# Two image layers on one core: VectorE in program order, loads a piece ahead, borders in the background, first group by channel pairs

## The chip, the cores and the metric

The kernel runs on one core of one Trainium2 chip. Its time is the device time of that core in microseconds; the median of three runs counts. TensorE (matmuls), VectorE, ScalarE (activations), GpSimd and SyncE (here it only issues DMA transfers) each work through a queue of their own.

## The reference

A batch of 32 images with 8 channels of 256 x 256 pixels, all f32, goes through two layers:

```python
def layer0(x):                      # x is normalised first: n = gn(x), 4 groups of 2 channels
    grid = n
    for _ in range(15):             # the "lattice": depthwise 3x3
        mapped = 3.9 * grid * (1 - grid)
        grid = 0.85 * (0.7 * mapped + 0.3 * conv3x3(mapped, K_local)) + 0.15 * n
    cml = clip(grid, 1e-4, 1 - 1e-4)
    h = relu(conv3x3(n, Wp, bp))    # 8 -> 128 channels
    nca = sigmoid(conv1x1(h, Wu, bu))
    g = relu(conv3x3(concat(n, cml, nca), Wg1, bg1))
    g = sigmoid(conv1x1(g, Wg2, bg2))
    return g * cml + (1 - g) * nca

y = x + layer0(gn(x))
qx = round(gn(y) * sx)              # sx = 127 / max|gn(y)|, over the whole batch
out = y + conv3x3(qx, qw) / (sx * sw) + bias
```

## The kernel before

Layer one works on groups of four images (`GB = 4`, eight groups). Four kinds of work run beside each other, and TensorE's order is written out by hand (each kind is a generator, and what it yields is its share of the time):

- **Preparation** (`normalise`, called by `prep`): a job is one image and two of its four channel pairs. `begin` loads each pair (`xr`, 512 KB) and takes its statistics at once (L305, L306); `scale` and `end` average them over the partitions with two small products on TensorE (`pm` L313, `pv` L324), get the deviation with a power on GpSimd (L327), normalise `xr` (L331), and make three copies: `xq` (ScalarE, L336), `hi` (VectorE, L342) and `lo` (GpSimd, L343). Six stores (L345, L352) write them at once to the scratch tensors `xq_s` and `xp_s`. One channel pair of one image is called a piece here. `hi`, `lo` and `xq` each have a single buffer, so each of them waits for the stores of the piece before.
- **Lattice** (`lattice`): for each of 8 channels, 15 steps of three tiles over the four images at once. A tile takes 12 products (L487) for two tensors, and on VectorE `gt` (L495) and the next `m_a` or `m_b` (L500). `m_a` gets rows of its neighbours with DMAs (`exchange`, L450, L451); `m_b`'s edge is masked on GpSimd (L504). The input of a channel comes from `xq_s` in 36 transfers (`load`).
- **NCA** (`nca`): per image, 3x3 products `ph` (L567), ReLU on ScalarE (L577), products `acc` (L584) and a sigmoid (L602), from `xp_s`, stored in `nc_s`.
- **Gate** (`gate`), one group behind: per image 10 pieces of two row blocks. `stage` loads `nb`, `cq` and `xb` (L671, L676, L690), rearranges `cq` to `cmb` on GpSimd (L681) and normalises `xb` to `xnb` on VectorE (L700); 18 products `pa` (L759), `pg` (L725), and `finish` with the gate's arithmetic (L730 to L735) and statistics (L743 to L745).

`together` emits one lattice step and then as much of the other three (the filler) as keeps both in proportion; `both` and `chain` mix the fillers. Before the first lattice, `prep(0, (0,))` prepares the first half (channel pairs 0 and 1) of four images; `prep(0, (1,))` follows beside the first lattice steps. The NCA of an image needs all its channels.

Only TensorE keeps this program order (L259). For VectorE, ScalarE, GpSimd and SyncE a planner sets the order at build time: it goes by the program's order among the instructions that it takes to be ready, by its own estimate of durations and transfers. On the chip each queue then runs in the order that was built.

Before all this, L194 to L202 store zeros to the border rows of 68 scratch tensors, four stores each, on ScalarE's DMA queue, from a tile `zt` in the pool `prep`. The pools of layer one (L261, L262) take over the space of `prep`. Layer two (L898 on) quantises the result and makes its convolution, image by image; the change doesn't touch it.

Of the kernel before, what the change touches and what calls it, by code (L numbers as in the profile page):

```python
# [31 lines left out]
F32 = mybir.dt.float32  # L32
# [8 lines left out]
P = 128  # L41
C = 8
# [71 lines left out]
def kernel(  # L114
# [46 lines left out]
    rstd_y = cp.tile([P, B], F32, name="rstd_y")  # L161
    dev_y = cp.tile([P, B], F32, name="dev_y")


# [7 lines left out]
    with tc.tile_pool(name="prep", bufs=1) as pp, tc.tile_pool(name="prep2", bufs=2) as pp2:  # L172
# [20 lines left out]

        zt = pp.tile([P, PW], F32, name="zt")  # L194
        G.memset(zt, 0.0)
        for t, n, w in (
            *((t, 2 * C, PW) for t in xp_s), *((t, C, W) for t in (*cm_s, *nc_s, *y_s))
        ):
            nc.scalar.dma_start(dram_ap(t, 0, [[w, n], [1, w]]), zt[:n, :w])
            for i in range(0, 11, 5):  # L200
                m = min(5, 11 - i) * n
                nc.scalar.dma_start(dram_ap(t, (257 + i) * n * w, [[w, m], [1, w]]), zt[:m, :w])  # L202

# [53 lines left out]
    with ExitStack() as one:  # L257

        one.enter_context(tc.manual_schedule(engines={mybir.EngineType.PE}))  # L259
        pool = lambda name, bufs, **kw: one.enter_context(tc.tile_pool(name=name, bufs=bufs, **kw))  # L260
        xp, sp2, gp, bp2, st = pool("xp", 4), pool("sp2", 1), pool("gp", 3), pool("bp2", 2), pool("st", 2)  # L261
        imp, hp, wk, wk1, np_ = pool("imp", 3), pool("hp", 12), pool("wk", 2), pool("wk1", 1), pool("np", 1)  # L262
        ps_c, ps_a = pool("ps_c", 6, space=PSUM), pool("ps_a", 2, space=PSUM)
# [24 lines left out]
        def normalise(jobs):  # L288

            def begin(b, half):
                xrs = []
                mv = st.tile([P, 2, 2], F32, name="mv", tag="mv")
                stats = st.tile([P, 2, 2, 6], F32, name="stats", tag="stats")
                for i in range(2):
                    g = 2 * half + i
                    xr = xp.tile([P, 2, 2, W], F32, name="xr", tag="xr")
                    nc.sync.dma_start(  # L300
                        xr.rearrange("p c h w -> p (c h) w"),
                        dram_ap(x, (b * C + 2 * g) * H * W, [[W, P], [P * W, 4], [1, W]]),
                    )
                    for j in range(2):
                        V.bn_stats(stats[:, i, j, :], xr[:, j].rearrange("p h w -> p (h w)"))  # L305
                    V.bn_aggr(mv[:, i, :], stats[:, i].rearrange("p j s -> p (j s)"))  # L306
                    xrs.append(xr)
                return b, half, xrs, mv

            def scale(b, half, xrs, mv):  # L310
                gs = slice(2 * half, 2 * half + 2)
                pm = ps_c.tile([P, 512], F32, name="pm", tag="pt")
                T.matmul(pm[:, 0:2], avg, mv[:, :, 0], start=True, stop=True)  # L313
                m, rstd = mean_x[:, b, gs], rstd_x[:, b, gs]
                V.tensor_copy(m, pm[:, 0:2])
                e = st.tile([P, 2], F32, name="e", tag="e")
                V.tensor_tensor(e, mv[:, :, 0], m, ALU.subtract)
                V.tensor_tensor(e, e, e, ALU.mult)
                V.tensor_tensor(e, e, mv[:, :, 1], ALU.add)
                return e  # L320

            def end(b, half, xrs, e):
                pv = ps_c.tile([P, 512], F32, name="pv", tag="pt")
                T.matmul(pv[:, 0:2], avg, e, start=True, stop=True)  # L324
                rstd = rstd_x[:, b, 2 * half : 2 * half + 2]
                V.tensor_scalar(rstd, pv[:, 0:2], GN_EPS, None, ALU.add)
                G.tensor_tensor(rstd, rstd, mhalf[:, 0:2], ALU.pow)  # L327
                for i, xr in enumerate(xrs):
                    g = 2 * half + i
                    flat = xr.rearrange("p c h w -> p (c h w)")  # L330
                    V.tensor_scalar(  # L331
                        flat, flat, mean_x[:, b, g : g + 1], rstd_x[:, b, g : g + 1],
                        ALU.subtract, ALU.mult,
                    )
                    xq = sp2.tile([P, 2, 2, 4, NJ], F32, name="xq", tag="xq")
                    S.activation(  # L336
                        xq.rearrange("p c h q j -> p (c h) q j"),
                        xr.rearrange("p c h (j q) -> p (c h) q j", q=4),
                        AF.Copy,
                    )  # L340
                    inner = lambda t: t[:, :, :, 1 : 1 + W]
                    V.tensor_copy(inner(hi), xr)  # L342
                    G.tensor_tensor(inner(lo), xr, inner(hi).bitcast(F32), ALU.subtract)  # L343
                    for h in range(2):
                        nc.sync.dma_start(  # L345
                            dram_ap(
                                xq_s[b % NBUF], (2 * g * H + P * h) * W, [[W, P], [H * W, 2], [1, W]]
                            ),
                            xq[:, :, h].rearrange("p c q j -> p c (q j)"),
                        )  # L350
                        for j, src in enumerate((hi, lo)):
                            nc.sync.dma_start(  # L352
                                dram_ap(
                                    xp_s[b % NBUF],
                                    (1 + P * h) * ROW + (C * j + 2 * g) * PW,
                                    [[ROW, P], [PW, 2], [1, PW]],
                                ),
                                src.bitcast(F32)[:, :, h, :],
                            )
                    yield 1.0  # L360
                ready.add((b, half))

            ahead = None
            for job in [*jobs, None]:
                now = begin(*job) if job else None
                yield 1.0
                if ahead:
                    e = scale(*ahead)
                    yield 1.0
                    yield from end(*ahead[:3], e)  # L370
                ahead = now

# [3 lines left out]
        def lattice(g):  # L376


            def load(u):


                c, out, dmas = u % C, [], []
                assert all((u // C * GB + i, c // 4) in ready for i in range(GB))
                for s in range(2):
# [57 lines left out]
            def background(n):  # L442
                for _ in range(min(n, len(later))):
                    nc.sync.dma_start(*later.pop(0))
                    issued[0] += 1

            def exchange(t, k):
# [109 lines left out]
        def nca(b):  # L557
# [80 lines left out]
            im = ahead  # L638
            if (b + 1, 0) in ready and (b + 1, 1) in ready:
                loaded[b + 1] = rows(b + 1, 0, 0)  # L640
# [26 lines left out]
        def stage(b, p, sc):  # L667
# [11 lines left out]
            )  # L679
            for k in range(n):  # L680
                G.tensor_copy(  # L681
                    cmb[:, k, 1 : 1 + W].rearrange("p (j q) -> p j q", q=4),
                    cq[:, k, :].rearrange("p (q j) -> p j q", q=4),
                )
            xb = bp2.tile([P, 2, W], F32, name="xb", tag="xb", bufs=3)
            if p in (0, 9):
                G.memset(xb, 0.0)
            for k in range(n):
# [6 lines left out]
                        [[W, r1_ - r0], [H * W, C], [1, W]],  # L695
                    ),
                )
            for k in range(n):
# [13 lines left out]
        def gate(b):  # L712
# [35 lines left out]
            last = done = None  # L748
            sc, ahead = staged.pop(b, None) or begin_gate(b)
            for p in range(10):  # L750
# [5 lines left out]
                for s, t in ((0, xnb), (1, cmb), (2, nb)):  # L756
# [11 lines left out]
                    if s < 2:  # L768
                        yield 2.6
                r1 = wk.tile([P, 512], F32, name="r1", tag="r1")  # L770
                S.activation(r1[:, : n * W], pa[:, : n * W], AF.Relu, bias=bv[:, 0:1])
# [93 lines left out]

        def prep(g, halves):
            return normalise([(b, half) for half in halves for b in range(g * GB, g * GB + GB)])

# [11 lines left out]
        T_NCA, T_GATE, T_PREP, T_LATTICE = 520.0, 340.0, 34.0, 8 * 45 * 1.97  # L880
        for _ in prep(0, (0,)):
            pass
        for g in range(NG):
            fill, t = images(nca, g), T_NCA
            if g:
                fill, t = both(fill, t, after(g - 1, images(gate, g - 1)), T_GATE), t + T_GATE
            if g + 1 < NG:
                fill, t = both(fill, t, prep(g + 1, (0, 1)), T_PREP), t + T_PREP
            if g == 0:
                fill, t = chain(prep(0, (1,)), fill), t + 20.0  # L890
            together(lattice(g), T_LATTICE, fill, t)
        for _ in images(gate, NG - 1):
            pass
# [115 lines left out]
```

## Time and profile before

| | |
|---|---|
| three runs | 14362.28, 14360.28, 14354.44 us |
| median | 14360.28 us |
| profiled run | 14414.7 us, mean TensorE clock 0.963 |

One run's profile is read here. Its first block gives the busy time of each engine. The second cuts the span in 40 slices of 360 us, with the busy tenths of each engine and the clock that TensorE was granted. The groups of instructions that matter for the change:

| group | count | mean ns | role |
|---|---|---|---|
| L487 `pt<-m_a`, `pt<-m_b` | 34560 | 497, 492 | lattice products |
| L567 `ph` | 24576 | 419, 402 | NCA products |
| L759 `pa` | 11520 | 588, 577, 576 | gate products |
| L495 `gt` | 5760 | 557, 549 | lattice, VectorE |
| L500 `m_a`, `m_b` | 5376 | 566, 575 | lattice, VectorE |
| L700 `xnb` | 608 | 493 | gate input, VectorE |
| L342 `hi` | 128 | 694 (median, first pieces) | preparation, VectorE |
| L343 `lo` | 128 | 2173 (median, first pieces) | preparation, GpSimd |

Matmuls overlap in the array, so the times of single ones add up to more than TensorE's busy time. Three more views are used: the chain of waits, which follows the work that ended last back from the end; the list of waits, which gives for each engine what ended its idle time (sum, times, longest); and a table of stretches of the run, with each engine's busy time, TensorE's clock and the DMA share in each.

### The profile page before, as it was taken

Reading aid. Unit: us, or ns where it says so; the run is one execution under the profiler, and the core shown is the slowest. Engines: PE = TensorE matmul, PEld = TensorE weight load, DVE = VectorE, ACT = ScalarE, POOL = GpSimd, SP = SyncE. Lnnn points to the kernel's source line nnn. Section 1 sums busy time; section 2 is a strip of 40 time slices with the busy share of each in tenths; the row PEclk is TensorE's granted clock in tenths of the full one; section 3 lists DMA queues with packets and bytes.
Section 4 is the critical chain, followed back from the end, with each engine's and each line's share of the span. In section 5 each row is a group of like instructions: output and inputs, shape, how many; then the busy total and the mean of one; then the engine's idle time right before and its main releaser. Section 6 shows DMA issues by size and latency. Waiting matters only on the chain.

```text
span 14414.7 us, 229163 instructions
## 1 busy us (share of the span) xinstructions
PE 13267.4 (92%) x81728; PEld 6423.3 (45%) x81728; DVE 8213.1 (57%) x16290; ACT 4039.8 (28%) x6274; POOL 2445.9 (17%) x4266
## 2 busy tenths in 40 slices
PE   2999999999999999999999999999999999999833
PEld 1554444444444444444444444444444444444311
DVE  3555555555555555555555555555555555555576
ACT  1333232232222222222322223222323222222122
POOL 1111111111111111111111111111111111112300
PEclk9999999999999999999999999999999999999966
DMA  5444444444444444444444434444444433333465
GB/s 148 93 97 92 90 103 106 103 94 100 110 94 100 99 106 94 103 100 95 100 103 107 98 93 106 110 94 94 104 104 98 103 88 88 80 83 78 122 195 176
DMA packets 2259559, 1496.74 MB, mean 104 GB/s; under 512 B 1061248, under 2 KB 2229504, under 8 KB 2258304
## 3 DMA queue, kind: packets, MB, share of 16 engines
q1 hardware_dynamic: 2176976, 1401.95, 41.9%
q10 hardware_dynamic: 81456, 80.12, 1.7%
q8 instruction: 664, 10.88, 0.3%
q14 instruction: 463, 3.79, 0.1%
HBM read 866.48 MB, written 478.69 MB: 93 GB/s over the span
## 4 chain that ended last, share of the span: by engine, by line
PE 70%; DMA 9%; DVE 9%; SPq 5%; issue 3%; POOL 2%; ACT 1%; ACTq 1%; POOLq 0%; DVEq 0%
PE pt L487 31%; PE ph L567 18%; PE pa L759 13%; PE acc L584 7%; DVE gt L495 2%; DMA im<-xp_s 1%; PE pg L725 1%; DMA xp_s<-lo 1%; SPq L545 1%; DVE m_b L500 1%; DMA xb<-in_x_dram 1%; DMA m_a<-m_a 1%; DMA out_dram<-ob 1%; SPq L960 1%; PE pt L953 1%
## 5 line engine op out<-in xcount | busy, mean ns | idle before, releaser
L487 PE MATMUL pt<-m_a,lw 128*64 128x390 f32 x17280 | 5827.0, 497 | 186.4 <-DMA m_a<-m_a 122.4
L487 PE MATMUL pt<-m_b,lw 128*64 128x384 f32 x17280 | 5796.6, 492 | 19.2 <-DVE m_b L410 18.0
L577 ACT ACTIVATE h<-ph,bp_sb 128x512 f32<-128x512 f32 x4096 | 2584.6, 684 | 6491.5 <-PE ph L567 6423.0
L487 PEld LDWEIGHTS pt<-m_a,lw 128*64 128x64 f32 x17280 | 2298.4, 138 | 1884.0 <-issue 1681.2
L487 PEld LDWEIGHTS pt<-m_b,lw 128*64 128x64 f32 x17280 | 2306.6, 138 | 1560.0 <-issue 1423.6
L567 PE MATMUL ph<-im,wp_hi 48*128 48x512 f32 x12288 | 2800.2, 419 | 174.2 <-DVE gt L495 113.1
L567 PE MATMUL ph<-im,wp_lo 48*128 48x512 f32 x12288 | 2675.2, 402 | 0.0
L495 DVE SCALAR_TENSOR_TENSOR gt<-pt,d_b 128x390 f32<-128x390 f32 x2880 | 1605.3, 557 | 1714.7 <-PE pt L487 1711.2
L495 DVE SCALAR_TENSOR_TENSOR gt<-pt,d_a 128x384 f32<-128x384 f32 x2880 | 1580.3, 549 | 1694.5 <-PE pt L487 1694.1
L504 POOL TENSOR_TENSOR m_b<-m_b,junk 128x12 f32<-128x12 f32 x2688 | 795.5, 296 | 8193.8 <-DVE m_b L500 7517.2
L567 PEld LDWEIGHTS ph<-im,wp_hi 48*128 48x128 f32 x12288 | 1417.5, 189 | 1081.7 <-DVE gt L495 303.9
L500 DVE SCALAR_TENSOR_TENSOR m_b<-gt 128x390 f32<-128x390 f32 x2688 | 1546.1, 575 | 44.5 <-DVE gt L495 2.3
L500 DVE SCALAR_TENSOR_TENSOR m_a<-gt 128x384 f32<-128x384 f32 x2688 | 1522.3, 566 | 17.2
L567 PEld LDWEIGHTS ph<-im,wp_lo 48*128 48x128 f32 x12288 | 1417.0, 189 | 217.3
L584 PE MATMUL acc<-h,wu_z 128*32 128x512 f32 x8320 | 1165.6, 603 | 6.1 <-ACT nca L602 5.5
L759 PE MATMUL pa<-xnb,gw 128*64 128x512 f32 (+1 forms) x3840 | 879.9, 588 | 43.7 <-DVE xnb L700 43.5
L759 PE MATMUL pa<-cmb,gw 128*64 128x512 f32 (+1 forms) x3840 | 857.6, 577 | 17.4 <-POOL cmb L681 17.4
L759 PE MATMUL pa<-nb,gw 128*64 128x512 f32 (+1 forms) x3840 | 863.6, 576 | 0.0
L730 POOL TENSOR_TENSOR d<-cmb,nb 128x512 f32<-128x512 f32 x320 | 502.9, 1572 | 1460.6 <-DVE gate L734 1028.5
L700 DVE TENSOR_SCALAR xnb<-xb,sc 128x256 f32<-128x256 f32 x608 | 290.7, 493 | 796.7 <-DMA xb<-in_x_dram 759.5
L953 PE MATMUL pt<-qt,qw 128*128 128x512 bf16 (+1 forms) x960 | 269.5, 451 | 477.0 <-ACT ob L954 425.4
L734 DVE TENSOR_TENSOR gate<-gate,d 128x512 f32<-128x512 f32 x320 | 217.4, 679 | 764.7 <-ACT gate L727 756.7
(132 smaller groups left out, 6928.0 us busy)
## 6 DMA issues: line engine op xcount, KB each, us to landing
im<-xp_s SPq DMA_DIRECT2D x1152, 193.5 KB
im<-xp_s SPq DMA_DIRECT2D x1216, 96.8 KB
d_a<-xq_s SPq DMA_DIRECT2D x2048, 36.0 KB
nb<-nc_s SPq DMA_DIRECT2D x288, 256.0 KB
cq<-cm_s SPq DMA_DIRECT2D x288, 256.0 KB
yb<-y_s ACTq DMA_DIRECT2D x29, 2432.0 KB
xb<-in_x_dram SPq DMA_DIRECT2D x544, 128.0 KB
xp_s<-hi SPq DMA_DIRECT2D x256, 258.0 KB
```

Of the source, the lines that this page charges most:

```text
L487: T.matmul(pt[half], lw[:, c, k, half], beside if part == 2 else own, start=part < 2, stop=part > 0,)
L495: V.scalar_tensor_tensor(gt, pt, FLOOR, d[:, ts, :], ALU.max, ALU.add)
L500: V.scalar_tensor_tensor(to, gt, 1.0, gt, ALU.subtract, ALU.mult)
L504: G.tensor_tensor(edge, edge, junk.unsqueeze(1).to_broadcast([P, 6, 2]), ALU.mult)
L567: T.matmul(ph[:, :n].rearrange("p (h w) -> p h w", w=W), w[64 * i : 64 * i + 48, dx, :], rhs[:, :, dx : dx + W], start=(dx == 0 and w is w ...
L577: S.activation(h[:, :n], ph[:, :n], AF.Relu, bias=bp_sb)
L584: T.matmul(acc[32 * g : 32 * g + 32, :cols], wu_z[:, 24 - 8 * i : 56 - 8 * i], h, start=first, stop=last,)
L700: V.tensor_scalar(xnb[:, k, 1 : 1 + W], xb[:, k, :], sc[:, i : i + 1], sc[:, 1:2], ALU.subtract, ALU.mult,)
L730: G.tensor_tensor(three(d), cmb[:, :n, 1 : 1 + W], nin, ALU.subtract)
L734: V.tensor_tensor(y[:, :cols], gt[:, :cols], d[:, :cols], ALU.mult)
L759: T.matmul(three[half], gw[:, s * 3 + dx, half], t[:, :n, dx : dx + W], start=(i == 0), stop=(i == 8),)
L953: T.matmul(pt, qw[:, dx, :], q[:, k0 : k0 + n, dx : dx + W], start=(dx == 0), stop=(dx == 2))
```

## The change

It has four parts. VectorE joins TensorE in keeping the program's order in layer one. So that it isn't held by a transfer, each load is taken apart from its first reader: `begin` only loads, `take` makes the statistics after the job before has ended; `stage` only loads, `arrange` makes `cmb` and `xnb` after the current piece's products; the stores of a prepared piece are issued when the next one begins (`pending`). The border stores, four per tensor, keep only those of the first four `xp_s` at the start; the others go to SyncE in places that the lattice's transfers leave free in the first group, and they read a 64-column `zt` in the constant pool repeatedly. The first group is prepared by channel pairs: one pair of each image ahead of the lattice, the other three beside it. The pools of layer one are opened in another order, and wait for reused space tile by tile.

```diff
+    zt = cp.tile([P, 64], F32, name="zt")
...
-        zt = pp.tile([P, PW], F32, name="zt")
         G.memset(zt, 0.0)
+        borders = []
         for t, n, w in (
-            *((t, 2 * C, PW) for t in xp_s), *((t, C, W) for t in (*cm_s, *nc_s, *y_s))
+            *((t, 2 * C, PW) for t in xp_s),
+            *((t, C, W) for t in (*nc_s[:GB], *cm_s[:GB], *nc_s[GB:], *cm_s[GB:], *y_s)),
         ):
-            nc.scalar.dma_start(dram_ap(t, 0, [[w, n], [1, w]]), zt[:n, :w])
-            for i in range(0, 11, 5):
-                m = min(5, 11 - i) * n
-                nc.scalar.dma_start(dram_ap(t, (257 + i) * n * w, [[w, m], [1, w]]), zt[:m, :w])
+            k = 64 if w == W else 43
+            for row, m in ((0, 1), (257, 5), (262, 5), (267, 1)):
+                borders.append(
+                    (
+                        dram_ap(t, row * n * w, [[w, m * n], [k, w // k], [1, k]]),
+                        zt[: m * n, :k].unsqueeze(1).to_broadcast([m * n, w // k, k]),
+                    )
+                )
+        for _ in range(4 * GB):
+            nc.scalar.dma_start(*borders.pop(0))
...
-        one.enter_context(tc.manual_schedule(engines={mybir.EngineType.PE}))
-        pool = lambda name, bufs, **kw: one.enter_context(tc.tile_pool(name=name, bufs=bufs, **kw))
-        xp, sp2, gp, bp2, st = pool("xp", 4), pool("sp2", 1), pool("gp", 3), pool("bp2", 2), pool("st", 2)
-        imp, hp, wk, wk1, np_ = pool("imp", 3), pool("hp", 12), pool("wk", 2), pool("wk1", 1), pool("np", 1)
+        one.enter_context(tc.manual_schedule(engines={mybir.EngineType.PE, mybir.EngineType.DVE}))
+
+        pool = lambda name, bufs, **kw: one.enter_context(
+            tc.tile_pool(name=name, bufs=bufs, reuse_waits="tile", **kw)
+        )
+        hp, xp, sp2, gp, bp2 = pool("hp", 12), pool("xp", 4), pool("sp2", 1), pool("gp", 3), pool("bp2", 2)
+        st, imp, wk, wk1, np_ = pool("st", 2), pool("imp", 3), pool("wk", 2), pool("wk1", 1), pool("np", 1)
...
-            def begin(b, half):
+            def begin(b, gs):
                 xrs = []
-                mv = st.tile([P, 2, 2], F32, name="mv", tag="mv")
-                stats = st.tile([P, 2, 2, 6], F32, name="stats", tag="stats")
-                for i in range(2):
-                    g = 2 * half + i
+                for g in gs:
                     xr = xp.tile([P, 2, 2, W], F32, name="xr", tag="xr")
                     nc.sync.dma_start(
...
+                    xrs.append(xr)
+                return b, gs, xrs
+
+            def take(b, gs, xrs):
+                mv = st.tile([P, 2, 2], F32, name="mv", tag="mv")
+                stats = st.tile([P, 2, 2, 6], F32, name="stats", tag="stats")
+                for i, xr in enumerate(xrs):
                     for j in range(2):
                         V.bn_stats(stats[:, i, j, :], xr[:, j].rearrange("p h w -> p (h w)"))
...
-                for i, xr in enumerate(xrs):
-                    g = 2 * half + i
+                for g, xr in zip(gs, xrs):
+                    if pending:
+                        stores(*pending.pop())
...
+                    pending.append((b, g, xq))
                     yield 1.0
...
             for job in [*jobs, None]:
                 now = begin(*job) if job else None
-                yield 1.0
+                yield 0.5
                 if ahead:
                     e = scale(*ahead)
                     yield 1.0
                     yield from end(*ahead[:3], e)
-                ahead = now
+                ahead = take(*now) if job else None
+                yield 0.5
+            stores(*pending.pop())
...
             def background(n):
                 for _ in range(min(n, len(later))):
                     nc.sync.dma_start(*later.pop(0))
+                    n -= 1
                     issued[0] += 1
+                if g == 0 and units.keys() - {0}:
+                    for _ in range(min(n, len(borders))):
+                        nc.sync.dma_start(*borders.pop(0))
...
-            for k in range(n):
-                G.tensor_copy(
-                    cmb[:, k, 1 : 1 + W].rearrange("p (j q) -> p j q", q=4),
-                    cq[:, k, :].rearrange("p (q j) -> p j q", q=4),
-                )
...
+            return xnb, xb, cmb, nb, cq, k0, n, sc
+
+        def arrange(xnb, xb, cmb, nb, cq, k0, n, sc):
+            for k in range(n):
+                G.tensor_copy(
+                    cmb[:, k, 1 : 1 + W].rearrange("p (j q) -> p j q", q=4),
+                    cq[:, k, :].rearrange("p (q j) -> p j q", q=4),
+                )
             for k in range(n):
                 i = 2 if k0 + k == 0 else 3 if k0 + k == NB - 1 else 0
...
-            sc, ahead = staged.pop(b, None) or begin_gate(b)
+            if b not in staged:
+                staged[b] = begin_gate(b)
+                yield 2.0
+                staged[b] = staged[b][0], arrange(*staged[b][1])
+            sc, ahead = staged.pop(b)
...
+                if p < 9:
+                    ahead = arrange(*ahead)
+                elif b + 1 in staged:
+                    staged[b + 1] = staged[b + 1][0], arrange(*staged[b + 1][1])
...
-        def prep(g, halves):
-            return normalise([(b, half) for half in halves for b in range(g * GB, g * GB + GB)])
+        def prep(g, groups=((0, 1), (2, 3))):
+            return normalise([(b, gs) for gs in groups for b in range(g * GB, g * GB + GB)])
...
-        for _ in prep(0, (0,)):
+        for _ in prep(0, ((0,),)):
             pass
...
             if g == 0:
-                fill, t = chain(prep(0, (1,)), fill), t + 20.0
+                fill, t = chain(prep(0, ((1,), (2, 3))), fill), t + 30.0
             together(lattice(g), T_LATTICE, fill, t)
+            while borders:
+                nc.sync.dma_start(*borders.pop(0))
```

## The prediction

> **What bounds the kernel now.** I read the page first, for the engine that is busy and where it is not.
>
> ```profile
> PE 13267.4 (92%) x81728; PEld 6423.3 (45%) x81728; DVE 8213.1 (57%) x16290; ACT 4039.8 (28%) x6274; POOL 2445.9 (17%) x4266
> ...
> PE   2999999999999999999999999999999999999833
> ...
> PEclk9999999999999999999999999999999999999966
> ...
> PE 70%; DMA 9%; DVE 9%; SPq 5%; issue 3%; POOL 2%; ACT 1%; ACTq 1%; POOLq 0%; DVEq 0%
> ```
>
> TensorE fills all slices but the first and the last three. So a change pays only where TensorE stands still or runs at a low clock. The chain of waits over the first 420 us shows the start:
>
> ```profile
> 112.47 1.33 DMA y_s<-zt
> 113.88 3.98 DMA xr<-in_x_dram
> ...
> 176.77 4.94 DMA xp_s<-lo
> 181.86 2.18 POOL lo L343
> ...
> 220.25 0.58 DVE m_b L410
> 220.87 8.32 PE pt L487 x34
> ...
> 310.06 5.93 DMA im<-xp_s
> 316.13 5.26 PE ph L567 x23
> ```
>
> The first load of `xr` is issued the moment the last border store has landed. TensorE's lattice starts at 220.9 us and its NCA work at 316. The table of stretches gives the rest (length, busy time of PE, PEld, DVE, ACT and POOL, then TensorE's clock and the DMA):
>
> ```profile
> 420.00:1600.00 1180.00, 1117.05 (x7262) 585.78 (x7260) 649.48 (x1334) 377.51 (x587) 124.16 (x300) 0.96 0.44 95
> 8267.00:9930.00 1663.00, 1620.25 (x10089) 788.16 (x10087) 957.55 (x1999) 477.54 (x744) 304.48 (x528) 0.98 0.44 100
> 11600.00:13212.00 1612.00, 1600.21 (x10088) 764.70 (x10086) 901.31 (x1890) 444.18 (x726) 269.18 (x510) 1.00 0.37 83
> 13212.00:13641.00 429.00, 390.02 (x1901) 144.83 (x1901) 224.23 (x471) 58.73 (x90) 172.39 (x185) 0.95 0.35 97
> 13641.00:14414.00 773.00, 269.49 (x960) 108.76 (x959) 521.10 (x203) 218.88 (x320) 0.38 (x1) 0.65 0.62 189
> ```
>
> A full group of four images takes some 1665 us with 43 us of TensorE idle at clock 0.98. The last group, which alone prepares no next group, has 12 us idle at clock 1.00 and takes 1612. So the preparation of `x` costs some 50 us a group, though its own matmuls take only some 5 (eight jobs, two products of 0.31 us each). Over 420 to 13212 us the same table sums to 330 us idle, and the missing clock (length times one minus clock, window by window) to some 210 us. The waits there:
>
> ```profile
> DVE xnb L700 <- DMA xb<-in_x_dram: 620.1, 220, 9.9
> DVE hi L342 <- DMA xp_s<-hi: 152.9, 40, 9.5
> DVE stats L305 <- DMA xr<-in_x_dram: 62.6, 27, 9.4
> ...
> PE pt L487 <- DMA m_a<-m_a: 115.4, 72, 6.5
> PE ph L567 <- DVE gt L495: 113.1, 151, 4.0
> PE pa L759 <- DVE xnb L700: 30.2, 5, 7.1
> ```
>
> VectorE waits for transfers for over 800 us, and TensorE then waits for VectorE or for the exchange behind it. I took every TensorE gap over 0.3 us and looked for a VectorE instruction that had been held over 1 us in the 6 us before: `hi` stands before 80 us of the gaps, `xnb` and `stats` before 86, none of these before 143.
>
> **What the Trainium skill says.** "PSUM — Partial Sum Buffer", section "Engine vs sequencer instructions": VectorE's queue is strictly first in, first out. The trace agrees: before the TensorE gap at 8394 us (5.75 us) VectorE sat 5.04 us at `xnb`, with `gt` behind it. "TensorE: Matmul & The Clock Gate", section "Part 1": an idle window of about 3.4 us drops TensorE to half clock, and it returns after as much sustained work. The trace agrees: after gaps of 2 to 4 us the lattice matmuls take 0.85 us in place of 0.49, and the clock lost (210) is 0.64 of the idle (330). So I price a microsecond of idle at 1.65 us.
>
> **The change part by part.**
>
> *Borders and the first load.* Before, 272 border stores sit on ScalarE's queue until 112 us, from a tile in the preparation pool whose space `xr` takes over. After, `zt` lies in the constant pool, 16 stores are issued at the start, the other 256 go to SyncE, and `hp` takes the old space. In the built order the four `xr` loads follow the constants directly (`bv` at 15.1 us before), so they land by some 20 to 25 us; VectorE's weight work (ends at 32 us) now comes first. I put the first `hi` at 36 us (before: 127): its statistics stand among the last weight operations, and its own chain (statistics to `hi`, 9.2 us before for two pieces) is some 6 us. The border rows become 256 or 172 bytes, 35,328 of them. Between 20 and 110 us the border queue took 23.9% of 16 engines for 8626 packets, that is 40 ns each (44 in the middle), so 97 us of all engines, spread over the first group: 9% on a DMA share of 0.44. I charge 15 us (0 to 40).
>
> *First group by channel pairs.* The lattice needs one piece of each image instead of two: 4 pieces rather than 8. A piece costs 8.9 us, the spacing of the `lo` lines above (2.2 on GpSimd, 1.5 of issue, 5 of landing, single buffers). Both kernels keep that chain. Lattice start: 36 + 3 x 8.9 + 3 (`lo`) + 28 (from the last `lo`'s end at 192.8 to the lattice at 220.9, the loads of `d_a`, `d_b`) = 94 us against 221. The twelve pieces left run beside lattice steps: 94 + 11 (one step, statistics) + 10 x 8.9 = 194 us for the start of the NCA work, which stands behind the last job's small matmuls on TensorE, against 316. By then six lattice steps of 6 us are done, before four: 12 us more. Together **-134 us** (-110 to -150).
>
> *VectorE in program order, loads ahead.* In the built order I counted lattice steps (13.4 us with their filler) between a load and its reader: `xb` to `xnb` a median of 0.0 before, 1.3 after; `xr` to `stats` 0 before, 12 after. With landings of 4 to 6 us these waits go, and their 86 us of gaps. `hi` is different: stores are now issued a piece later, so in 14 of 24 pieces that I followed they stand in the same step as the `hi` that waits for them (before, mostly one step or more ahead). That `hi` can wait some 7 us (five issues of 0.5, landing 4 to 5). But it stands after the step's last `m_a`, with only gate work and the next step's `gt` behind it; TensorE then has some 7 us of filler and three tiles of 2 us for which six PSUM buffers are free. I keep half of the 80 us. Of the 143 others, mostly late exchanges, stores that wait for `lo` no longer hold SyncE's queue in front of them; the last group shows that a group without pieces has 12 of 42 us left. I take a quarter, 35 us. So 86 + 40 + 35 = 161 us idle, times 1.65 = 266.
>
> *Against it:* in order, `m` follows its own `gt` at 0.59 us instead of 0.47 with another between. Six pairs a step make 0.7 us on VectorE, which is busy 57%; slack hides it except in steps with little filler: 10 us. With the borders' 15, the middle comes to **-240 us** (0 to -360).
>
> *The last gates.* TensorE is busy 390 of 429 us, so a piece is bound by its own 8.6 us of matmuls. Loads ahead save the wait for `xnb` at image borders: **-10 us** (0 to -25). The second layer's 773 us keep their order: nothing.
>
> Sum: 134 + 240 + 10 = 384; 14360 - 384 = **13976, say 13980 us**.
>
> **The rivals.** *Preparation disappears whole:* six groups fall from 1665 to some 1620 (270), the first middle stretch loses its 63 idle and 47 clock but for 20 (90), the start 134, the tail 15: 13850. For it: the clean last group. Against: the stores in the same step. *The middle only trades waits:* `hi`, the gate's product (already 743 us at ScalarE's `gate`) and the small statistics now hold a queue that can't be rearranged; what loads ahead win is lost there. Only start and tail remain: 14360 - 144 = 14215. For it: `hi`'s place, and that the scheduler's order could put ready work first. *Slower:* 65 pieces hold VectorE 6 us each, two thirds reach TensorE, times 1.65 = 430, less the start, tail and the 142 for `xnb` and `stats`: +144, 14500. Against it: filler and PSUM buffers as above, and only 80 of 220 us of such waits reached TensorE before.
>
> **How the numbers follow.** Forecast 0.52, whole gain 0.22, traded waits 0.20, slower 0.06. The range goes from 13840, a little below the whole gain, to 14210, about the traded waits. Faster 0.93, same 0.01, slower 0.06.
>
> **What would show it.** Start: an `xr` load before 25 us, first lattice matmul near 94 us, first NCA matmul near 194. Middle: `xnb` and `stats` gone from VectorE's DMA waits, `hi` still there with 150 to 400 us; groups of 1625 to 1640 us, idle of some 25, clock 0.99. Wrong if the `xr` loads still wait for other space, if pieces come slower than 8.9 us because border packets crowd them, or if `PE <- DVE gt` grows because `hi` or `gate` holds the queue.

## The result: slower, and the profile after

The changed kernel takes 14551.9 us (median of four runs) against 14357.4 us of the kernel before on the same chip, a ratio of 1.0133 (95% interval 1.0116 to 1.0151). The forecast was 13980. Chips differ by up to 0.4% here for the same kernel, so below I compare ratios, each to the kernel before on the same chip, and turn them into microseconds with 14360. The two profiled executions lie only 108 us apart (14522.4 and 14414.7): a comparison of their marks shows the direction and rather too little of the size.

The page of the changed kernel, the lines that answer to those shown of before (busy time; TensorE and its clock in 40 slices; the chain by engine):

```profile
PE 13336.1 (92%) x81744; PEld 6386.4 (44%) x81744; DVE 8724.6 (60%) x16310; ACT 4048.1 (28%) x6274; POOL 2226.0 (15%) x4270
...
PE   5889999999999999999999999999999999999833
...
PEclk8999999999999999999999999999999999999966
...
PE 75%; DVE 8%; DMA 7%; SPq 5%; issue 2%; ACT 1%; POOL 0%; POOLq 0%; DVEq 0%; ACTq 0%
```

The first slice fills from 2 to 5 tenths: the start works. But slices 2 and 3, which were at 9, are at 8, and VectorE is busy 8725 us in place of 8213 for almost the same instructions (16310 and 16290). The last group of experiments shows where that comes from. The first run of lattice matmuls and the first NCA matmuls, from the timeline of TensorE (start, length, line, what, idle before). Two single lattice matmuls come 20 us ahead of the run, here and in the kernel before (201.3 us there):

```profile
100.59 1.55 PE L515 MATMUL pt<-m_b,lw 128*64 128x384 f32 x4 [18.53 <-DVE m_b L434]
...
230.83 0.80 PE L595 MATMUL ph<-im,wp_hi 48*128 48x512 f32 x2
```

The lattice starts at 100.6 us instead of 220.9 (I had said 94), the NCA work at 231 instead of 305 to 316 (I had said 194). The table of stretches, columns as before:

```profile
420.00:1600.00 1180.00, 1049.52 (x6630) 561.20 (x6628) 639.34 (x1221) 344.51 (x536) 87.86 (x273) 0.93 0.42 92
3265.00:4930.00 1665.00, 1610.82 (x9980) 771.25 (x9976) 1009.06 (x1980) 472.08 (x737) 275.57 (x523) 0.98 0.43 99
11600.00:13212.00 1612.00, 1597.88 (x10121) 761.84 (x10119) 962.24 (x1908) 451.89 (x732) 246.97 (x513) 1.00 0.37 85
```

The stretch from 420 to 1600 us has 130 us of TensorE idle at clock 0.93; before it had 63 at 0.96. A middle stretch of 1665 us has 54 idle, before 43. Counted from lattice matmul to lattice matmul, the second group starts at 1702 us (before 1681), so the 120 us won at the start are gone before the first group ends, and a middle group takes some 1680 us (before some 1665; forecast 1625 to 1640). The waits from 300 to 13200 us (in total, times, longest):

```profile
PE ph L595 <- DVE gt L523: 230.6, 184, 7.2
PE pt L515 <- DMA m_a<-m_a: 88.8, 62, 5.1
PE pa L794 <- DVE xnb L731: 44.7, 23, 5.2
PE pg L756 <- DVE gt L523: 33.8, 6, 5.9
...
DVE hi L380 <- DMA xp_s<-hi: 572.0, 66, 14.2
```

`xnb` and `stats` are gone from VectorE's waits for transfers, as forecast. But `hi` waits 572 us where it waited 161 (153 in the window that the prediction shows), and TensorE's wait for `gt` has doubled (113 us before). Counted as in the prediction, between 420 and 13212 us, a held `hi` now stands ahead of 241 us of TensorE's gaps; before it was 80.

One `hi` shows how. SyncE's queue (an exchange, loads for the next channel, then the stores of the piece before):

```profile
3944.90 0.58 SPq L479 DMA_DIRECT2D m_a<-m_a  x1
3945.52 0.44 SPq L468 DMA_DIRECT2D d_a<-xq_s  x1
3946.07 2.14 SPq L468 DMA_DIRECT2D d_b<-d_a  x2
3948.25 2.01 SPq L340 DMA_DIRECT2D xq_s<-xq  x2
3950.62 0.36 SPq L346 DMA_DIRECT2D xp_s<-hi  x1
3951.09 0.60 SPq L346 DMA_DIRECT2D xp_s<-lo  x1
3951.75 0.52 SPq L346 DMA_DIRECT2D xp_s<-hi  x1
```

VectorE at the same time, and then TensorE:

```profile
3943.49 0.80 DVE L369 TENSOR_SCALAR xr<-xr,mean_x,rstd_x 128x1024 f32<-128x1024 f32 x1
3958.10 0.69 DVE L380 CAST hi<-xr 128x1024 fp32r<-128x1024 f32 x1 [13.80 <-DMA xp_s<-hi]
3958.70 0.55 DVE L523 SCALAR_TENSOR_TENSOR gt<-pt,d_a 128x384 f32<-128x384 f32 x1
```

```profile
3959.31 1.97 PE L756 MATMUL pg<-r,gw 128*64 128x512 f32 x4 [5.85 <-DVE gt L523]
```

`xr` is scaled by 3944.3, but `hi` may only overwrite its buffer when the store of the last piece's `hi` has landed. That store was held back until this piece began and is issued at 3951.75, behind an exchange and two `d_b` loads, and lands near 3958. For 13.8 us nothing moves on VectorE; the `gt` of the next step stand behind `hi`, no PSUM buffer comes free, and TensorE stops for 5.85 us.

### The profile page after: what moved, and what is told of

It is laid out like the page before. It is cut to its first block, busy times and chain, and to the rows that moved or that the text cites. A ratio compares the mean times of both kernels' runs of the same rounds, so it can differ in the third digit from the quotient of the medians.

```text
span 14522.4 us, 227774 instructions
## 1 busy us (share of the span) xinstructions
PE 13336.1 (92%) x81744; PEld 6386.4 (44%) x81744; DVE 8724.6 (60%) x16310; ACT 4048.1 (28%) x6274; POOL 2226.0 (15%) x4270
## 4 chain that ended last, share of the span: by engine, by line
PE 75%; DVE 8%; DMA 7%; SPq 5%; issue 2%; ACT 1%; POOL 0%; POOLq 0%; DVEq 0%; ACTq 0%
PE pt L515 31%; PE ph L595 19%; PE pa L794 15%; PE acc L612 7%; DVE gt L523 3%; DVE m_a L528 2%; DMA xp_s<-hi 2%; PE pg L756 1%; DMA im<-xp_s 1%; DMA out_dram<-ob 1%; SPq L468 1%; DMA yb<-y_s 1%; PE pt L994 1%; SPq L573 1%; SPq L1001 1%
## 5 line engine op out<-in xcount | busy, mean ns | idle before, releaser
L532 POOL TENSOR_TENSOR m_b<-m_b,junk 128x12 f32<-128x12 f32 x2688 | 585.8, 218 | 8637.6 <-DVE m_b L528 8311.9
L528 DVE SCALAR_TENSOR_TENSOR m_b<-gt 128x390 f32<-128x390 f32 x2688 | 1590.6, 592 | 227.8 <-DVE gt L523 6.0
L528 DVE SCALAR_TENSOR_TENSOR m_a<-gt 128x384 f32<-128x384 f32 x2688 | 1581.9, 589 | 92.5
L810 ACT ACTIVATE r<-pa,bv 128x512 f32<-128x512 f32 x320 | 213.0, 666 | 1867.1 <-PE pa L794 1866.6
```

The costliest lines, as they stand in the source:

```text
L528: V.scalar_tensor_tensor(to, gt, 1.0, gt, ALU.subtract, ALU.mult)
L532: G.tensor_tensor(edge, edge, junk.unsqueeze(1).to_broadcast([P, 6, 2]), ALU.mult)
```

## The experiments

Theory A: the late stores make `hi` hold VectorE's fixed queue. Theory B: the fixed order costs by itself. Theory C: the borders on SyncE crowd the first group. "us" is the ratio times 14360.

| run | edit to the changed kernel, unless it says before | ratio (95%) | us |
|---|---|---|---|
| change | | 1.0133 (1.0116-1.0151) | 14551 |
| e1_once | stores at once | 0.9904 (0.9889-0.9918) | 14222 |
| e1_half | stores half a step later | 0.9932 (0.9917-0.9947) | 14262 |
| e2_twohi | two `hi` | 0.9892 (0.9878-0.9907) | 14205 |
| e4_planner | VectorE planned | 0.9867 (0.9851-0.9884) | 14169 |
| e5_bdve | before + VectorE in program order | 1.0427 (1.0410-1.0445) | 14973 |
| e6_start | before + start part | 0.9938 (0.9924-0.9953) | 14271 |
| e7_spread | borders spread | 1.0107 (1.0090-1.0124) | 14514 |
| e7_planner_spread | planned, borders spread | 0.9845 (0.9830-0.9860) | 14137 |
| e8_planner_once | the last, stores at once | 0.9829 (0.9816-0.9843) | 14114 |
| e8_planner_twohi | planned, borders spread, two `hi` | 0.9807 (0.9794-0.9821) | 14083 |
| e9_twohi_spread | borders spread, two `hi` | 0.9863 (0.9850-0.9877) | 14163 |
| e10_pairs | the last, both `gt` ahead of both `m` | 0.9752 (0.9739-0.9765) | 14004 |
| e11_pairs_only | both `gt` ahead of both `m` | 0.9974 (0.9963-0.9985) | 14323 |
| e12_once_pairs | stores at once, spread, both `gt` first | 0.9780 (0.9766-0.9795) | 14044 |
| e13_planner_pairs | planned, spread, two `hi`, both `gt` first | 0.9798 (0.9783-0.9812) | 14070 |

**The stores of `hi` (e1_once, e1_half, e2_twohi).**

```diff
-                    if pending:
-                        stores(*pending.pop())
...
-                    pending.append((b, g, xq))
+                    stores(b, g, xq)          # e1_once
                     yield 1.0
```

> Changed kernel, but the six stores of a piece are put into the program straight after hi and lo are made, as in the kernel before, and not when the next piece begins. Theory A (late stores: hi holds VectorE's fixed queue because the stores that read the old hi are put off until the next piece begins): hi's wait for its store falls from 572 us to below 250, the matrix-multiply groups' wait for gt from 232 us to about 110, and the time falls by about 170 us of idle time and as much again by 0.7 in clock, to some 14270 us. Theory B (the fixed order itself costs, stores or not): 14500 to 14600 us, with the idle time behind gt unchanged. Theory C (border packets crowd the first group): no change outside the first group, 14500 us.

For e1_half the last two lines are `yield 0.5`, `stores(b, g, xq)`, `yield 0.5`.

> Changed kernel with the stores of a piece put into the program half a filler step after hi and lo are made: by then lo is done, so SyncE need not wait for it, and the next hi is still at least half a filler step away. Theory A: the least waiting of the three placements, hi's wait below 200 us, 14200 us or a little less, below the variant that stores at once. Theory B: 14500 to 14600 us. Theory C: 14500 us.

```diff
-        hi, lo = fixed([P, 2, 2, PW], "hi", F32R), fixed([P, 2, 2, PW], "lo", F32R)
+        his = [fixed([P, 2, 2, PW], f"hi{i}", F32R) for i in range(2)]
+        lo, turn = fixed([P, 2, 2, PW], "lo", F32R), [0]
...
+                    hi = his[turn[0] % 2]
+                    turn[0] += 1
...
-                    pending.append((b, g, xq))
+                    pending.append((b, g, xq, hi))
```

`cq` and `r1` also go down to one buffer each here, and in every later run with two `hi`.

> Changed kernel with two buffers for hi that take turns, the stores put off as in the changed kernel; to make room the arranged-column buffer cq and the gate's r1 have one buffer instead of two. VectorE then never waits for the store of the piece just made, while lo's wait stays, on GpSimd. Theory A: hi's wait goes from 572 us to below 50 and the groups that wait for gt lose some 200 us of idle time, 14200 us. Theory B: 14500 to 14600 us. Theory C: 14500 us.

The wait of `hi` is gone altogether in e1_once and e2_twohi (2.7 us are left in e1_half). The waits of TensorE from 300 to 13200 us, first e1_once, then e2_twohi:

```profile
PE pt L512 <- DMA m_a<-m_a: 128.4, 73, 5.5
PE ph L592 <- DMA im<-xp_s: 60.6, 32, 7.2
PE ph L592 <- DVE gt L520: 58.7, 126, 2.0
```

```profile
PE pt L518 <- DMA m_a<-m_a: 99.2, 65, 6.3
PE ph L598 <- DVE gt L526: 80.3, 150, 3.0
...
PE ph L598 <- DMA im<-xp_s: 35.6, 24, 6.5
```

Two edits that have nothing in common but that `hi` no longer waits win 329 and 346 us. So Theory A holds, and its cost is larger than the whole loss. Stores at once have a price too, on the exchange and the image rows (29 and 25 us more wait than with two buffers). My guess that half a step later would be best was wrong: there `m_a` waits 163 us. Where in the step those stores meet the exchanges I did not follow up.

**The order of VectorE (e4_planner, e5_bdve).**

```diff
-        one.enter_context(tc.manual_schedule(engines={mybir.EngineType.PE, mybir.EngineType.DVE}))
+        one.enter_context(tc.manual_schedule(engines={mybir.EngineType.PE}))      # e4_planner
```

> Changed kernel with VectorE's order left to the planner again (only TensorE keeps the program's order); late stores, loads ahead, borders and channel pairs stay. Theory A: the planner places hi by its own reckoning of when the buffer is free, so the late stores cost less: the groups' wait for gt near the 113 us of the kernel before, 14250 us. Theory B: as much, 14250 us or below, since the fixed order is what costs. Theory C: 14500 us, as the borders stay.

e5_bdve is the opposite edit, on the kernel before.

> Kernel before with one edit: VectorE too keeps the program's order in layer one, nothing else of the change. Theory A (a fixed queue is paid for by each wait that stands in it): nothing is loaded ahead here, so the bn_stats wait for the load issued just ahead of them, and xnb for its own; the stores go out at once, so hi waits little. Several hundred us of such waits stand in the queue, gt behind them: 14550 to 14900 us. Theory B (the loads ahead matter little; the program's order itself is good or bad): within 50 us of the kernel before, or 14200 us.

The waits of e4_planner, from 300 to 13200 us:

```profile
PE ph L595 <- DVE gt L523: 52.8, 68, 2.3
...
DVE xnb L731 <- DMA xb<-in_x_dram: 568.7, 204, 12.4
DVE hi L380 <- DMA xp_s<-hi: 244.3, 52, 11.4
```

and of e5_bdve:

```profile
DVE xnb L700 <- DMA xb<-in_x_dram: 1105.7, 186, 17.1
...
DVE stats L305 <- DMA xr<-in_x_dram: 94.8, 15, 11.3
```

The fixed order without loads ahead costs 613 us, more than the range that I gave; with everything else of the change it costs 382 us (e4 to the change). The planned kernel still has 813 us of waits at `xnb` and `hi`, yet TensorE's wait for `gt` is 53 us: what a wait costs depends on what stands behind it. Under the planner that is less often what TensorE needs next; in the program's order it is the next `gt`.

**The start and the borders (e6_start, e7_spread, e7_planner_spread).** e6_start is the kernel before with `zt` kept, the borders in the background and the first group by channel pairs; `take` follows `begin` at once, `arrange` is part of `stage`, the stores go out at once in the order that the change gives them.

> Kernel before with the start of the change alone: borders in the background, the first group by channel pairs, zt kept. VectorE is planned, the stores go out at once, nothing is loaded ahead. The prediction's step for the start gives 134 us: 14230 us, the lattice 120 us earlier, and all later marks too. Theory C (the borders, at about 0.8 us of SyncE's queue each, and the pieces now beside the first group give most of it back before the group ends): the lattice starts 120 us earlier but its second group only 20 to 50 us earlier, 14310 to 14340 us.

The two others spread the borders:

```diff
-                if g == 0 and units.keys() - {0}:
-                    for _ in range(min(n, len(borders))):
+                if units.keys() - {0}:
+                    for _ in range(min(n, 1, len(borders) - (0 if g else 4 * (B + 3 * GB)))):
                         nc.sync.dma_start(*borders.pop(0))
```

with the borders sorted so that the 80 needed first stand first.

> Changed kernel with the borders spread thinner: in the first group only the 80 or so that it and the next need, at most one to a tile of the lattice and not three, the other 176 in the second group, one to a tile. VectorE's fixed order and the late stores stay. Theory C: the first group's idle time falls by some 40 us and its clock rises, 60 us in all, 14490 us. Theory A: the stores' place in SyncE's queue improves only where borders stood ahead of them, 14500 to 14540 us, and hi still waits over 450 us. Neither holds if it is above 14550 us.

> Changed kernel with VectorE planned (as in the run before of that kind, ratio 0.987 to the kernel before) and the borders spread as in the run beside it. Theory C: 60 us below that, ratio 0.983, 14115 us; the first group's end comes at about 1580 us and not 1629 us. If borders cost nothing: ratio 0.987, 14170 us.

SyncE's queue in the changed kernel, in the first group:

```profile
611.43 0.83 SPq L473 DMA_DIRECT2D nc_s<-zt  x1
612.37 0.62 SPq L478 DMA_DIRECT2D m_a<-m_a  x1
613.05 0.58 SPq L479 DMA_DIRECT2D m_a<-m_a  x1
613.67 2.32 SPq L473 DMA_DIRECT2D nc_s<-zt  x3
616.11 0.61 SPq L478 DMA_DIRECT2D m_a<-m_a  x1
...
629.86 6.17 SPq L473 DMA_DIRECT2D cm_s<-zt  x8
636.14 0.61 SPq L478 DMA_DIRECT2D m_a<-m_a  x1
```

Borders take about 0.75 us of the queue each. Where no exchange is put in between, eight of them hold it for 6.2 us, and the exchange at 636 us starts behind them.

e6_start gains 89 us (67 to 109), not 134. Its lattice starts 108 us earlier, its second group only 32 us earlier (1649 us); the rest comes in later groups, which are some 15 us shorter each (the chip of the trace of before, 0.4% slower, makes some 7 of that), perhaps from the new order of the stores; I did not separate that. Spreading the borders is worth 37 us in the changed kernel and 32 under the planner (and 42 with two `hi`, e2_twohi to e9_twohi_spread); the intervals of the first two pairs overlap a little, but the three agree, and so do the marks: the first group ends at 1624 instead of 1702 us, and at 1583 instead of 1629. In the changed kernel the second group, which then has the other borders, gives 48 of the 78 us back. e7_spread is 24 us above what I expected from Theory C and inside the range for Theory A, whose wait of `hi` stays (585 us). So Theory C holds, as the smallest of the causes. The Trainium skill ("Perfetto Trace Analysis", section "DMA Optimizations") says that spreading transfers over the engines that can issue them may help where the issuing engine is what is full; borders on ScalarE's queue beside the first group were not tried.

**What is left under the planner (e8_planner_once, e8_planner_twohi, e9_twohi_spread).** These combine edits shown above.

> VectorE planned, borders spread, and the stores of a piece put into the program at once, not late. Against the run with VectorE planned and borders spread but late stores (0.9845 of the kernel before). If late stores cost only under a fixed order, the two are the same within 0.2 per cent, 14100 to 14160 us on the scale of the kernel before at 14360. If late stores cost under the planner too (hi still waited 222 us there): 0.980 or less. If late stores pay under the planner, because SyncE is not held by stores that wait for lo: 0.988 or more.

> VectorE planned, borders spread, late stores, two buffers for hi (cq and r1 with one each). If hi's 222 us of waits that are left under the planner cost TensorE anything, this is below 0.9845 of the kernel before, 0.982 or so; if the planner already puts hi where nothing urgent stands behind it, 0.984 to 0.986.

> VectorE in the program's order, late stores, two buffers for hi, borders spread: the changed kernel with both costs taken away. The terms add: 0.9892 for two buffers of hi, less 0.0024 for the borders, 0.987, 14170 us. Under the planner it would then still be 0.0025 or 35 us better: that is what the fixed order itself costs once no wait stands in it. If 0.985 or below, the fixed order costs nothing by itself.

Stores at once or late are the same under the planner within what can be told (0.9829 against 0.9845, intervals overlapping). A second `hi` takes 0.0038 off: `hi`'s wait falls to 64 us, so even the planner's places for it seem not to have been free. And e9 against e8_planner_twohi, which differ in the order of VectorE alone, are 80 us apart. (The 35 us that I expected was reckoned from 0.9845, the planned kernel with one `hi`.) Without any wait of `hi`, the fixed order as written still costs something; the next group shows what.

**Each `m` behind its own `gt` (e10_pairs, e11_pairs_only, e12_once_pairs, e13_planner_pairs).**

```diff
+                        jobs_gt = []
                         for s, a2b, n, pt in jobs:
                             gt = gp.tile([P, 6 * (NJ + 1)], F32, name="gt", tag="gt")
...
                             V.scalar_tensor_tensor(gt, pt, FLOOR, d[:, ts, :], ALU.max, ALU.add)
+                            jobs_gt.append(gt)
+                        for (s, a2b, n, pt), gt in zip(jobs, jobs_gt):
+                            d = ds[s][1 if a2b else 0]
                             if step == STEPS - 1:
```

> As the run with VectorE in the program's order, two buffers for hi and the borders spread (0.9863 of the kernel before), with one edit: in each lattice tile both gt are made ahead of both m, so that no m stands straight behind the gt that it reads. Theory B1 (what the fixed order itself costs is mainly that each m starts 0.1 to 0.2 us late behind its own gt): the idle time ahead of the m instructions falls from some 315 us to below 70 and the ratio to 0.981 to 0.983, 14090 to 14115 us on the scale of 14360. Theory B2 (it is the places of the gate's and the pieces' instructions between the tiles, which the planner chooses by what is late): the idle time ahead of m falls as much and the ratio stays at 0.985 to 0.988.

> The changed kernel with one edit: both gt of a lattice tile ahead of both m. Late stores, one hi, the borders as in the change. If the two causes add: 1.0133 less 0.0111, so 1.002 of the kernel before, 14390 us, with hi still waiting over 500 us. If the m were only worth something once hi no longer held the queue: 1.009 or more. If m behind gt was the main cause and hi follows from it: 0.99 or less.

> The changed kernel with the stores at once, the borders spread, and both gt ahead of both m; one hi, and all buffers as they were. If stores at once do what a second hi does: 0.990 less 0.0025 less 0.011, so 0.9765, 14020 us. If SyncE, held by stores that wait for lo, still costs beside the second buffer: 0.978 to 0.980, with longer waits of the matrix multiplies for m_a and im than the variant with two buffers had (95 and 25 us).

> VectorE planned, two buffers for hi, borders spread (0.9807 of the kernel before), and both gt ahead of both m in the program. If the planner already sets such pairs apart (some 60 us of idle time ahead of m are left there): no change, 0.980 to 0.982. If its order follows the program enough to gain: 0.977 or less.

VectorE in the changed kernel, two pairs from its timeline:

```profile
3962.66 0.55 DVE L523 SCALAR_TENSOR_TENSOR gt<-pt,d_a 128x384 f32<-128x384 f32 x1
3963.24 0.56 DVE L528 SCALAR_TENSOR_TENSOR m_a<-gt 128x384 f32<-128x384 f32 x1
3963.72 0.56 DVE L523 SCALAR_TENSOR_TENSOR gt<-pt,d_b 128x390 f32<-128x390 f32 x1
3964.38 0.56 DVE L528 SCALAR_TENSOR_TENSOR m_b<-gt 128x390 f32<-128x390 f32 x1
```

An `m` starts 0.58 or 0.66 us after its `gt`, and what does not depend on the one ahead of it 0.48 us after. (The Trainium skill, "VectorE: DVE Perf Modes", section "The DRAIN you can't avoid", says that the next instruction does not start until the pipe is empty, that one which is not held starts earlier, and that in a chain of copies a semaphore after each costs nothing extra. The trace fits the second: the independent one starts before the 0.55 us of the one ahead are over. The one that reads the result starts 0.10 to 0.18 us later than that, a price that the chain of copies there doesn't show.) The groups by line, from 300 to 13000 us (busy, mean ns, then the idle time ahead of them), in the kernel before:

```profile
L500 DVE SCALAR_TENSOR_TENSOR m_b<-gt 128x390 f32<-128x390 f32 x2626 | 1509.8, 575 | 43.7 <-DVE gt L495 2.3
L500 DVE SCALAR_TENSOR_TENSOR m_a<-gt 128x384 f32<-128x384 f32 x2626 | 1484.5, 565 | 16.9
```

in the changed kernel:

```profile
L528 DVE SCALAR_TENSOR_TENSOR m_b<-gt 128x390 f32<-128x390 f32 x2574 | 1520.6, 591 | 219.1 <-DVE gt L523 6.0
L528 DVE SCALAR_TENSOR_TENSOR m_a<-gt 128x384 f32<-128x384 f32 x2575 | 1516.7, 589 | 88.6
```

and in e11_pairs_only:

```profile
L532 DVE SCALAR_TENSOR_TENSOR m_b<-gt 128x390 f32<-128x390 f32 x2614 | 1514.0, 579 | 0.0
L532 DVE SCALAR_TENSOR_TENSOR m_a<-gt 128x384 f32<-128x384 f32 x2614 | 1510.0, 578 | 0.0
```

The idle time ahead of `m` is 308 us in the changed kernel, 61 before, none with both `gt` first. With that edit VectorE's busy time, in which an overlap of two instructions counts once, also goes back to that of the kernel before, as the page of e11_pairs_only shows:

```profile
PE 13294.1 (93%) x81744; PEld 6406.6 (45%) x81744; DVE 8259.8 (57%) x16310; ACT 4053.0 (28%) x6274; POOL 2458.2 (17%) x4270
```

The edit alone takes the changed kernel from 1.0133 to 0.9974, 228 us, and wins 159 us where `hi` has two buffers. Both are more than I expected (1.002, and 0.981 at best), and the costs don't simply add: this one is larger where `hi` still waits. Under the planner the edit changes nothing (0.9798 against 0.9807), but there it hardly reached the order that was built: 60 us of idle time ahead of `m` stay, as without it. The planner had set such orders by itself, in the kernel before too (`gt`, `gt`, `m`, `m` three times from 8387.3 to 8393.2 us). So it is the fixed order, as the program wrote it, that brings this cost in. The waits of e10_pairs, from 300 to 13200 us, show where TensorE gets part of it back:

```profile
PE pt L518 <- DMA m_a<-m_a: 94.9, 62, 6.2
...
PE ph L602 <- DVE gt L527: 23.5, 33, 3.0
```

The wait for `gt` is 23.5 us, a tenth of what it is in the changed kernel (79 in e9). Two things come together in this edit, and I can't tell them apart: `m` no longer waits for its `gt`, and the second `gt`, which frees a PSUM buffer, no longer stands behind the first `m`. e12, with stores at once, is at 0.978, a little above e10 as its second expectation said (`m_a` 116 us, `im` 41). e10_pairs is the best version here: 2.5% below the kernel before, with VectorE in the program's order. It differs from e13_planner_pairs in the order of VectorE alone and is 66 us faster, with intervals that don't overlap (0.9739 to 0.9765, 0.9783 to 0.9812). So a fixed order is not worse in itself: it cost what its own places of `hi` and `m` cost, and without these it beats the planner's.

## Why the prediction was wrong

- **The step that failed is "I keep half of the 80 us" for `hi`.** The place was right and the length of one wait nearly: "some 7 us", measured 8.7 on average (572 / 66), though 572 us in all against the "150 to 400" I gave. The argument that filler and six PSUM buffers would hide it was wrong: behind `hi` stood the next step's `gt`, ready, and TensorE ran out of PSUM buffers. The gaps behind `hi` grew from 80 to 241 us, and taking the wait away wins 329 to 346 us. Expected was a gain of 40 x 1.65 = 66.
- **"`m` follows its own `gt`: 10 us"** is a term that was mis-sized: 159 to 228 us (with the earlier second `gt` in it, which the runs don't separate). I had the 0.59 us right and took VectorE's 57% busy time for slack. But TensorE waits for a certain `gt` at a certain moment (its PSUM buffers come free by them), and an average share says nothing of that.
- **The borders' 15 us** were too few: spreading them out alone wins 32 to 42, and what they cost in all was not measured. I counted their packets on the DMA engines; the trace shows them on SyncE's queue, at about 0.75 us an issue for some 240 of them, with exchanges behind them.
- **The start's -134 us** came to a lattice start 120 us earlier, as said, but NCA work at 231 and not 194 us: pieces beside the lattice take 11.4 us (twelve `hi` from 115.9 to 241.0 us) and not the 8.9 us that I took over from pieces alone. Of the gain at the start, the start part alone keeps 32 us at the end of the first group. With borders spread and `hi` and `m` mended (e10_pairs) the second group starts at 1571 us, 110 us earlier than before.
- **"`xnb` and `stats` go, 86 us"** was right in the waits. What it won can't be told: under the planner, loads ahead, late stores and the new pools together win 102 us (e6_start 0.9938 to e4_planner 0.9867), against 142 that I put on the first alone, and there `xnb` still waits 569 us.
- **"A quarter" of the 143 us of other gaps** did not go. Counted the same way, the gaps with no held `hi`, `xnb` or `stats` before them are 211 us in the changed kernel and 210 in e10_pairs.
- **That e10_pairs comes near the forecast is in part luck.** It is at 0.9752, 14004 us; the sum of the prediction was 13976. But in e10_pairs `hi` never waits and no `m` follows its `gt`, and for such a kernel the prediction's own terms give 13976 - 66 - 10 = 13900. So the gains are some 100 us smaller than I put them, and real: the three costs, 547 us from the change to e10_pairs, had more than eaten them. I had them at 25 us of cost and a gain of 66.
- **The price of 1.65 for a microsecond of idle** held roughly: between 420 and 13212 us TensorE was idle 470 us and lost 328 us of clock in the changed kernel, 217 and 116 in e10_pairs, which makes 1.70 and 1.54. The low clock comes sooner than the window of 3.4 us that I cited for it: after the gap of 2.57 us at 8383.5 us, in the kernel before, lattice matmuls already take 0.86 us.
- **The rival "slower" (14500, chance 0.06)** came nearest: "65 pieces hold VectorE 6 us each, two thirds reach TensorE"; it is 66 waits of 8.7 us, of which 0.43 reach TensorE as gaps (241 of the 562 us between 420 and 13212 us). It left out `m` and borders. I gave it too little because I read its evidence off the kernel before, where the planner had chosen what stands behind `hi`: that 80 us of such waits reached TensorE there is no measure of a fixed order. The statement of the Trainium skill that VectorE's queue is strictly first in, first out ("PSUM — Partial Sum Buffer", section "Engine vs sequencer instructions") agrees with the trace of the changed kernel (13.80 us with a ready `gt` behind `hi`); I drew too small a conclusion from it. The gap at 8394 us that I gave for it does not show such a case: there TensorE waited for `xnb` itself, which its next products read, and the next `gt` ran only at 8411.6 us, 2.2 us after the first of its own products.

## What to carry to other kernels

Before an engine's order is fixed, list every instruction on it that can wait for a transfer and what would stand behind it; price the wait by that, and not by what the same wait cost while a planner chose the place. A transfer that reads a single buffer must be issued as early as the next writer needs, or the buffer doubled; and in a fixed order independent instructions go between a producer and its reader. An issue on a shared queue is priced by its time on that queue, beside its packets.

## What was not expected of the hardware

- Waits of 569 and 244 us on VectorE (e4_planner) in a kernel that takes 2.6% less time than one with 572 us at `hi` alone (the change).
- A border store of 8 to 40 KB holds SyncE's queue about 0.75 us (2.32 us for three), longer than an exchange (0.6).
- A VectorE instruction that reads the result of the one ahead starts 0.1 to 0.2 us later than one that doesn't. On an engine 60% busy, setting an independent one between (which also moved the second `gt` ahead) was worth 1.1 to 1.6% of the whole time.
